# Mamba's gate: SiLU of z per channel tile, tanh on ScalarE and two GpSimd operations at written-out slots

## The chip, the core and the metric

The program runs on one core of a Trainium2 chip. The metric is the device time of one execution in microseconds (us); of the kernel before, the median of three runs is taken. The profile is one further execution with every instruction recorded. The engines are named as in the profile: PE (TensorE), with its weight loads as PEld; DVE (VectorE); ACT (ScalarE); POOL (GpSimd); and SP (SyncE), which issues the DMAs.

## The reference, cut to what matters

The input x has 64 x 64 positions (4096 tokens) of 256 channels, in float32. Three layers follow one another: a convolution and attention block, a bidirectional Mamba block with an MLP behind it, and a block of experts; each is added to its input. The change is in the second:

```python
def _mamba(x, ...):                       # once forward, once on the reversed tokens
    xz = einsum('bld,ed->ble', x, in_proj_w)
    xc, z = split(xz, 2, axis=-1)         # 512 channels each
    xc = silu(causal_conv(xc, conv_w, 4 taps) + conv_b)
    x_dbl = einsum('bld,ed->ble', xc, x_proj_w)    # dt (16), B (16 states), C (16)
    dt = softplus(einsum('blr,dr->bld', dt, dt_proj_w) + dt_proj_b)
    dA = exp(dt[..., None] * A)
    dBx = dt[..., None] * Bm[:, :, None, :] * xc[..., None]
    h_t = dA_t * h_{t-1} + dBx_t ;  y_t = sum over states of h_t * C_t
    y = y + xc * Dp
    y = y * silu(z)
    return einsum('bld,ed->ble', y, out_proj_w)

m = fwd + bwd
h = layernorm(m) * ln_g + ln_b
t = t + m + leaky_relu(h @ w1.T + b1, 0.01) @ w2.T + b2
```

silu(z) = z * sigmoid(z), which equals z/2 + z/2 * tanh(z/2).

## The kernel before, in words

The program has one phase for each layer. `mamba_phase` is the second and runs from about 2044 us to 4046 us of the span.

**Chunks and slots.** The 4096 tokens are cut into eight stretches of 512 (N), and each is gone through forward and backward, so there are 16 chunks, i = 0 to 15; even ones are forward (d = 0), odd ones backward (d = 1). A channel tile is 128 of the 512 channels (e = 0 to 3). The 16 states are cut into four quads (k). One tile of the scan has 128 partitions (32 channels by 4 states) and 2 x 512 elements. A chunk therefore has 4 (e) x 4 (k) x 2 (j) = 32 slots, and the phase 512. `at` is the slot's number in its chunk, 0 to 31.

**The order.** Everything in the phase is emitted in one written-out order: a loop over the slots emits, for slot n, its instructions to all engines, and each engine runs its own in that order and waits by semaphore for what it needs. Per slot n there are
- `inflow(n + 2)` on POOL (L1669): the product of dt*x and B for the slot two ahead, into one of three `dbx` buffers;
- `keep(n - 1)` on ACT (L1700): the last column of the scan before is copied out as state;
- `decay(n + 1)` on ACT (L1659): two exp of 128 x 512 into one of two PSUM buffers `da`;
- `bring(n + 1)` on ACT (L1692): from chunk 2 on, the state brought over from the chunk before is added to the first column of `dbx`;
- `recur(n)` on DVE: the scan (L1677) in place on `da`, and the product h with C (L1682);
- every second slot, `sum_states` on PE (L1709): the sums over states into `y`; at slots 8, 16, 24 and 0, `close` on DVE (L1717): y times silu(z) into the tile that held xc.

**Beside the slots.** `output` projects the finished chunk at slots 1 to 3 (L1434 on PE; ACT copies the result for forward chunks, L1439, and DVE adds it for backward ones, L1441). At slot 0 of a chunk ACT runs SiLU over its z, two tiles of 128 x 1024 (L1777); for chunk 0 this is done at the start (L1585).

`prepare(q)` is a generator that makes the inputs of the next chunk, one step a slot: the in-projection of xc (`in_pair`, PE L1250) at slots 29 and 30, copies on ACT (L1277, L1281) at 30 and 31, the four taps as matmuls (PE L1294) at slots 3 to 6, their bias on ACT (L1290) at 4 to 7, one SiLU over the whole xc at slot 8 (L1298), the projections to B, C and dt, an exp at slot 16, a log at slot 23 (L1342), and at slots 24 to 29 the pieces of dt on POOL: L1365 an addition and L1376 a product, each 128 x 512, whose results SP stores (L1380). The projections of z run at slots 24 and 26, and ACT copies them out of PSUM at 25 and 27 (L1355; for chunk 0 L1570). At slot 27 SP issues the load of the next chunk's input u (`load_u`, L1259). The last two pieces of dt come at slots 2 and 4 of the next chunk. SP issues every DMA of these in program order; `load_dt` fetches dt rows for the next channel tile (L1419).

`tail(c)` is a generator for one finished pair of chunks: LayerNorm (PE L113 and L122, DVE L116, ACT, POOL L132 and L138), an addition on POOL (L1457), the MLP (PE L1465, ACT, DVE L1471, PE L1476, DVE L1481), and the store with the token sums. It advances by at most one step a slot, and only if the slot is not in the set `FULL` of the engine that the step uses.

`few` is a ring of three 128 x 512 buffers; z tiles have three buffers of 128 x 1024.

Of the kernel before, what the change touches and what calls it, by code (L numbers as in the profile page):

```python
# [18 lines left out]
AF = mybir.ActivationFunctionType  # L19
ALU = mybir.AluOpType  # L20
# [1146 lines left out]
def mamba_phase(cx, early, w_in, w_x, w_out, w1, w2, x1d, ud, bcd, dtd, x2d, u2d, usum):  # L1167
# [11 lines left out]
    nc, tc = cx.nc, cx.tc  # L1179
    with ExitStack() as ctx:  # L1180
# [60 lines left out]
        def mm_psum():  # L1241
            return pmm.tile([P, N], FP, name="mm", tag="mm")
# [13 lines left out]
        def load_u(i):  # L1256
            c, d = divmod(i, 2)
            u = early.new_u()
            nc.sync.dma_start(out=u, in_=ud[NCH - 1 - c if d else c])  # L1259
            gots[i] = {"u": u}  # L1260

        def in_pair(q, e):
            return [in_proj(q % 2, gots[q]["u"], e), in_proj(q % 2, gots[q]["u"], e + 1)]

        def few():
            return sp.tile([P, N], FP, name="few", tag="few", bufs=3)

        def prepare(q):

            d, got = q % 2, gots[q]  # L1270

            ps = in_pair(q, 0)
            yield
            xp = early.wide("xp")
            nc.scalar.copy(xp[:, :, 0:3], halo[d])
            for v in range(2):
                nc.scalar.copy(xp[:, v, 3:], ps[v])  # L1277
            ps = in_pair(q, 2)
            yield
            for v in range(2):  # L1280
                nc.scalar.copy(xp[:, 2 + v, 3:], ps[v])  # L1281
            nc.scalar.copy(halo[d], xp[:, :, N : N + 3])
            for _ in range(4):
                yield

            xc = None
            for e in range(ET + 1):
                if e > 0:
                    xc = got["xc"] = xc or pr.tile([P, ET, N], FP, name="xc", tag="xc")
                    nc.scalar.activation(xc[:, e - 1, :], ps, AF.Identity, bias=cx.col(f"convb{d}", e - 1))  # L1290
                if e < ET:
                    ps = mm_psum()
                    for k in range(4):
                        nc.tensor.matmul(  # L1294
                            ps, taps[d][:, 4 * e + k, :], xp[:, e, k : k + N], start=k == 0, stop=k == 3
                        )
                yield
            nc.scalar.activation(xc, xc, AF.Silu)  # L1298
            yield
            ps = mm_psum()  # L1300
            nx = DR + 2 * DS
            for e in range(ET):
                nc.tensor.matmul(ps[0:nx, :], wx[d][:, e, :], xc[:, e, :], start=e == 0, stop=e == ET - 1)
            yield
            xd = few()[0:nx, :]
            nc.scalar.copy(xd, ps[0:nx, :])

            at = 0 if d else DR
            nc.sync.dma_start(out=bcd[q], in_=xd[at : at + 2 * DS, :])
            yield  # L1310


            r = slice(32 * d, 32 * d + DR)
            ex = dt = None
            for e in range(ET + 1):
                if e > 0:
                    ex = early.wide("ex")[:, :, 0:N] if e == 1 else ex
                    dt = dt or sp.tile([P, ET, N], FP, name="dt", tag="dt")
                    nc.scalar.activation(ex[:, e - 1, :], ps, AF.Abs, bias=cx.col(f"dtb{d}", e - 1))
                    nc.scalar.activation(dt[:, e - 1, :], ps, AF.Relu, bias=cx.col(f"dtb{d}", e - 1))  # L1320
                if e < ET:
                    ps = mm_psum()
                    nc.tensor.matmul(ps, wdt[r, P * e : P * e + P], xd[r, :], start=True, stop=True)
                yield

            nc.scalar.activation(ex, ex, AF.Exp, scale=-1.0)
            yield
            rds, sums = {}, {}
            for e in range(ET + 2):
                if e < ET:  # L1330
                    rd = rds[e] = few()
                    nc.scalar.activation(rd, ex[:, e, :], AF.Identity, scale=-1.0, bias=-1.0)
                    nc.scalar.add(rd, rd, 1.0)
                if e > 1:
                    nc.scalar.copy(dt[:, e - 2, :], sums.pop(e - 2))
                if 0 < e <= ET:
                    ps = sums[e - 1] = mm_psum()
                    for v, x in enumerate((rds.pop(e - 1), ex[:, e - 1, :], dt[:, e - 1, :])):
                        nc.tensor.matmul(ps, cx.ident, x, start=v == 0, stop=v == 2)
                yield  # L1340

            nc.scalar.activation(ex, ex, AF.Ln, bias=1.0)  # L1342
            yield
            got["dt"] = dt
            for at, (v, e) in enumerate(((0, 0), (1, 0), (0, 1), (1, 1), (0, 2), (0, 3))):
                dt_piece(q, v, e, ex)
                if at == 4 and q > 1:
                    load_first(q, 0)
                if at in (0, 2):
                    zs = in_pair(q, ET + at)  # L1350
                if at in (1, 3):
                    z = sp.tile([P, 2, N], FP, name="z", tag="z", bufs=3)
                    got.setdefault("z", []).append(z)
                    for f in range(2):
                        nc.scalar.copy(z[:, f, :], zs[f])  # L1355
                if at == 3 and q + 1 < 2 * NCH:
                    load_u(q + 1)
                yield

        def dt_piece(q, v, e, ex=None, eng=nc.gpsimd):  # L1360


            dt, xc = gots[q]["dt"], gots[q]["xc"]
            if v == 0:
                eng.tensor_tensor(dt[:, e, :], dt[:, e, :], ex[:, e, :], ALU.add)  # L1365
                if q < 2:
                    return
                if e == 0:
                    firsts[q] = ip.tile([P, ET], FP, name="first", tag="first", bufs=1)
                nc.gpsimd.tensor_tensor(firsts[q][:, e : e + 1], dt[:, e, 0:1], odd[:, 0:1], ALU.add)  # L1370
                if e % 2:
                    first_rows[q, e // 2] = cx.rows.tile([P, 2], FP, name="first_row", tag="first_row", bufs=2)
                    nc.sync.dma_start(out=first_rows[q, e // 2], in_=firsts[q][:, e - 1 : e + 1])
            else:
                x = few()
                eng.tensor_tensor(x, dt[:, e, :], xc[:, e, :], ALU.mult)  # L1376

                eng.tensor_tensor(dt[:, e, 0:1], dt[:, e, 0:1], odd[:, 1:2], ALU.add)
                for w, piece in enumerate((dt[:, e, :], x)):
                    nc.sync.dma_start(out=dtd[2 * q + w][e].rearrange("p j n -> (p j) n"), in_=piece)  # L1380

        def load_first(q, h):

# [107 lines left out]
        def start():  # L1491


            got, xp = gots[0], early.xp
# [42 lines left out]
            for v in range(2):  # L1537
                dt_piece(0, v, 0, ex, nc.vector)
# [19 lines left out]
            zs = in_pair(0, ET)  # L1558
# [7 lines left out]
            for h in range(2):  # L1566
                z = sp.tile([P, 2, N], FP, name="z", tag="z", bufs=3)
                got.setdefault("z", []).append(z)
                for f in range(2):
                    nc.scalar.copy(z[:, f, :], zs[f])  # L1570
                if h == 0:
                    zs = in_pair(0, ET + 2)
                    for v in range(2):
                        dt_piece(0, v, 1, ex)
                    yield
# [5 lines left out]
            yield  # L1581
            dt_piece(0, 1, 2)
            yield
            for z in got["z"]:
                nc.scalar.activation(z, z, AF.Silu)  # L1585
            dt_piece(0, 0, 3, ex)
            load_u(1)
            yield
# [60 lines left out]
        gots, bcs, dts, m_of, das, us, ys, hs = {}, {}, {}, {}, {}, {}, {}, {}  # L1649
# [65 lines left out]
        def close(i, e):  # L1715
            g, z = gots[i]["xc"], gots[i]["z"]
            nc.vector.tensor_tensor(g[:, e, :], ys.pop((i, e)), z[e // 2][:, e % 2, :], ALU.mult)  # L1717

        there = set()
        CARRY = {30: (0, 0), 31: (0, 2), 9: (1, 0), 11: (1, 2)}  # L1720

        AHEAD = 3
# [2 lines left out]

        FULL = {
            "PE": {0, 1, 2, 3, 4, 5, 6, 7, 9, 18, 19, 20, 21, 24, 26, 29, 30},
            "ACT": {0, 6, 7, 8, 16, 17, 18, 19, 20, 21, 22, 23, 30, 31},
            "POOL": {0, 1, 2, 4, 24, 25, 26, 27, 28, 29, 30, 31},
            "DVE": {8, 16},  # L1730
            "DMA": {},
        }
# [1 line left out]
        with tc.manual_schedule(engines=ORDERED):  # L1734
# [5 lines left out]
            for n, (i, e, k, j) in enumerate(slots):  # L1740
                at = n % SPS
                if at == 0:
                    prep, coming = coming, None
                if at in CARRY and 1 < i + (at > 16) < 2 * NCH:
                    carry(i + (at > 16), *CARRY[at])
                inflow(n + 2)
# [22 lines left out]
                if 1 <= at <= 3 and out is not None:  # L1769
                    step(out)  # L1770
                    if at == 3:
                        out = None
                        if (i - 1) % 2:
                            tails.append(tail((i - 1) // 2))
                if at == 0 and i > 0:
                    for z in gots[i]["z"]:
                        nc.scalar.activation(z, z, AF.Silu)  # L1777
                if i == 0:
                    step(begin)
                step(prep, LATE.get(at, 1) if i == 0 else 1)  # L1780
# [340 lines left out]
```

## Time and profile before

| | |
|---|---|
| runs | 4381.84 us median of 3 (4381.3 to 4389.78) |
| profiled execution | 4368.56 us, span 4366.8 us, mean granted PE clock 0.904 |
| phases in the span | convolutions to 760 us, attention to 2044, Mamba to 4046, experts to the end |
| Mamba window, 2002 us: busy | DVE 1893.0, PE 1619.0, ACT 1451.4, POOL 1449.4 |
| scan L1677 (512) and product L1682 (512) | 2.350 us and 1.225 us each |
| inflow L1669 (512), decay L1659 (1024) | 2.360 us on POOL, 0.692 us on ACT |
| SiLU of z: L1777 | 30 activations of 1.049 us, 15 table loads of 1.283 us |
| closing product L1717 (64) | 0.681 us |

Rows of a group of instructions read: line, engine, operation, out<-in with partitions x elements, count | busy us, mean ns of one | idle time of the engine in front of them and what ended it. Rows of the timeline read: start us, duration us, engine, line, operation, and in brackets the idle time just before and what ended it. Rows of waits read: who waited <- what ended the wait: us in total, times, longest us. Rows of windows read: window, its length, and the busy time of PE, PEld, DVE, ACT and POOL with their instruction counts, the granted PE clock, the DMA share and GB/s.

### The profile page before, as it was taken

To read this page: it belongs to the slowest core of one execution; us is meant where nothing else is said; L and a number is where in the kernel's file an instruction comes from. 1 tells how busy PE (TensorE), PEld (TensorE's weight loads), DVE (VectorE), ACT (ScalarE), POOL (GpSimd) and SP (SyncE) were. 2 spreads that over 40 slices of the span, in tenths; PEclk is the share of its full clock that TensorE was granted. 3 is DMA by queue.
4 is the path that set the end of the run, shared out by engine and by line. 5 is a ranking of instruction groups with operands and counts; after the bars stand their busy time and mean duration, and the time that the engine had idled before them with its cause. 6 is when DMAs were issued, how large, how long until landed. Compare 5 with 4: busy or idle time off the path is not lost. (4 is left out here: it accounts for less than half of the span.)

```text
span 4366.8 us, 43278 instructions
## 1 busy us (share of the span) xinstructions
PE 3693.8 (85%) x15072; PEld 1180.6 (27%) x15072; DVE 3600.9 (82%) x2976; ACT 2685.7 (62%) x4175; POOL 1563.3 (36%) x1051
## 2 busy tenths in 40 slices
PE   4659895999999999997878788888788788876698
PEld 2224341222222222222222222222222222221243
DVE  6887876888879879778899999999999999999311
ACT  1012223888788888776677777777777777774122
POOL 2210000000000000002677677776767777776000
PEclk9879996999999999998888989989888898977799
DMA  4322223000000000003332334443323334332121
GB/s 148 125 77 93 75 79 129 4 30 11 25 23 18 16 23 18 11 23 118 104 108 98 103 124 119 123 119 107 127 82 124 124 114 118 120 109 84 63 63 37
DMA packets 150243, 351.18 MB, mean 80 GB/s; under 512 B 35461, under 2 KB 44421, under 8 KB 149502
## 3 DMA queue, kind: packets, MB, share of 16 engines
q1 hardware_dynamic: 139214, 313.17, 23.1%
q0 software_dynamic: 10800, 35.14, 2.3%
q8 instruction: 120, 1.97, 0.2%
q14 instruction: 109, 0.89, 0.1%
HBM read 268.69 MB, written 79.56 MB: 80 GB/s over the span
## 5 line engine op out<-in xcount | busy, mean ns | idle before, releaser
L1669 POOL TENSOR_TENSOR dbx<-dtxr,b 128x1024 f32<-128x1024 f32 x512 | 1205.8, 2360 | 467.7 <-DVE da L1677 320.7
L1677 DVE TENSOR_TENSOR_SCAN da<-da,state,dbx 128x1024 f32<-128x1024 f32 x512 | 1203.2, 2350 | 62.0 <-ACT state L1700 33.6
L960 ACT ACTIVATE e<-sc 128x1024 f32<-128x1024 f32 x1024 | 992.8, 1023 | 204.7 <-PE sc L953 161.2
L881 DVE TENSOR_TENSOR s<-s,e 128x1024 f32<-128x1024 f32 x768 | 880.6, 1216 | 44.7 <-ACT e L960 44.2
L1659 ACT ACTIVATE da<-dtr,aneg 128x512 f32<-128x512 f32 x1024 | 708.3, 692 | 36.0 <-DMA dtr<-dtd 3.8
L953 PE MATMUL sc<-q,kS 32*128 32x512 f32 x4096 | 653.6, 644 | 20.4 <-DMA kS<-kd 11.4
L1682 DVE TENSOR_TENSOR h<-da,c 128x1024 f32<-128x1024 f32 x512 | 627.2, 1225 | 37.7
L888 PE MATMUL av<-e,vT 128*32 128x512 f32 x4096 | 549.8, 608 | 3.7 <-ACT o L894 3.7
L1709 PE MATMUL y<-h,sel 128*32 128x512 f32 x2048 | 442.0, 675 | 130.9 <-DVE h L1682 130.7
L132 POOL TENSOR_TENSOR ln_few<-ln_few,minus_half 128x4 f32<-128x4 f32 x29 | 29.4, 1015 | 1417.8 <-DMA ln_few<-ln_row 1417.8
L452 PE MATMUL cv<-v,u 128*128 128x512 f32 x928 | 422.2, 615 | 64.4 <-DVE pad L272 27.4
L953 PEld LDWEIGHTS sc<-q,kS 32*128 32x128 f32 x4096 | 211.3, 183 | 466.9 <-issue 244.4
L1250 PE MATMUL mm<-u,win 128*128 128x512 f32 x496 | 267.2, 688 | 72.0 <-DMA u<-ud 52.4
L1700 ACT COPY state<-da 128x2 f32<-128x2 f32 x511 | 80.5, 158 | 362.5 <-DVE h L1682 360.0
L452 PEld LDWEIGHTS cv<-v,u 128*128 128x128 f32 x928 | 182.1, 198 | 302.9 <-issue 230.9
L528 DVE SCALAR_TENSOR_TENSOR acc<-pad,wdw_s,acc 128x768 f32<-128x768 f32 (+1 forms) x192 | 244.5, 1279 | 19.4 <-ACT acc L524 13.3
L1294 PE MATMUL mm<-xp,taps 128*128 128x512 f32 x480 | 221.3, 609 | 6.0 <-DVE m L1441 5.1
L881 DVE TENSOR_TENSOR s<-e 128x1024 f32<-128x1024 f32 x128 | 150.8, 1219 | 71.6 <-ACT e L960 71.4
L888 PEld LDWEIGHTS av<-e,vT 128*32 128x32 f32 x4096 | 81.3, 108 | 396.6 <-issue 379.0
L1709 PEld LDWEIGHTS y<-h,sel 128*32 128x32 f32 x2048 | 60.4, 114 | 468.5 <-DVE h L1682 292.8
L1250 PEld LDWEIGHTS mm<-u,win 128*128 128x128 f32 x496 | 104.2, 221 | 244.8 <-issue 127.0
L504 ACT COPY pad<-pad 128x480 f32<-128x480 f32 x12 | 7.1, 594 | 214.2 <-DVE pad L272 214.1
(338 smaller groups left out, 3747.3 us busy)
## 6 DMA issues: line engine op xcount, KB each, us to landing
dtr<-dtd SPq DMA_DIRECT2D x128, 512.0 KB
dtxr<-dtd SPq DMA_DIRECT2D x128, 512.0 KB
b<-bcd SPq DMA_DIRECT2D x64, 256.0 KB
c<-bcd SPq DMA_DIRECT2D x64, 256.0 KB
dtd<-dt SPq DMA_DIRECT2D x64, 256.0 KB
dtd<-few SPq DMA_DIRECT2D x64, 256.0 KB
u<-uv SPq DMA_DIRECT2D x24, 640.0 KB
u<-ud SPq DMA_DIRECT2D x16, 512.0 KB
```

The source lines that it names most:

```text
L452: nc.tensor.matmul(rows4(ps), u[:, dy, P * ci : P * ci + P], v[:, dy : dy + HR, ci, :], start=dy + ci == 0, stop=dy == k - 1 and ci == CT - 1,
L528: nc.vector.scalar_tensor_tensor(o, src, w_ap, o, ALU.mult, ALU.add)
L881: nc.vector.tensor_tensor(z, x, y, ALU.add)
L888: nc.tensor.matmul(g.av[32 * h : 32 * h + 32, :], vT[:, kb, P * t + 32 * h : P * t + 32 * h + 32], es[h // 2][:, h % 2, :], start=kb == 0, ...
L953: nc.tensor.matmul(ps[h // 2][:, h % 2, :], kS[r, t, P * kb : P * kb + P], q_t[r, t, :], start=True, stop=True,)
L960: nc.scalar.activation(e, ps[i], AF.Exp)
L1250: nc.tensor.matmul(ps, win[d][:, t, P * e : P * e + P], u[:, t, ::-1] if d else u[:, t, :], start=t == 0, stop=t == CT - 1,)
L1659: nc.scalar.activation(da[:, v, :], dts[i, e, j][0][:, v, :], AF.Exp, scale=aneg[i % 2][:, a : a + 1])
L1669: nc.gpsimd.tensor_tensor(u, dts[i, e, j][1], bcs[i, k][0][:, None, :].to_broadcast([P, 2, N]), ALU.mult)
L1677: nc.vector.tensor_tensor_scan(da, da, u, state[i % 2][:, 4 * e + j, k : k + 1], ALU.mult, ALU.add)
L1682: nc.vector.tensor_tensor(h, da, bcs[i, k][1][:, None, :].to_broadcast([P, 2, N]), ALU.mult)
L1709: nc.tensor.matmul(ys[i, e][32 * j : 32 * j + 32, :], cx.sel, hs[n + j // 2][:, j % 2, :], start=False, stop=k == SQ - 1,)
```

## The change

z is halved as it is copied out of PSUM: `scalar.mul` by 0.5 in the place of `scalar.copy`, in `prepare` and for chunk 0. The two SiLU activations at slot 0 of every chunk, and those of chunk 0, are gone. In their place `swish` makes silu(z) from z/2 for one channel tile at a time, at fixed slots: tanh of 128 x 512 on ACT into a `few` buffer at slots 4, 11, 13 and 21; the product of it with z/2 on POOL at slots 6, 12, 15 and 22; and the addition of z/2 on POOL, into z, at slots 7, 14, 16 and 23. In a slot these come behind the inflow, the decays and the scan of the slot. The sets `FULL` change: ACT's free slots now include 0 and no longer 4, 11 and 13, and POOL's no longer 6, 7, 14, 15 and 22.

```diff
@@ prepare, and the start of chunk 0
                     for f in range(2):
-                        nc.scalar.copy(z[:, f, :], zs[f])
+                        nc.scalar.mul(z[:, f, :], zs[f], 0.5)
@@ new
+        def swish(i, at):
+
+            e, part = SWISH[at]
+            z = gots[i]["z"][e // 2][:, e % 2, :]
+            if part == 0:
+                tanhs[i, e] = few()
+                nc.scalar.activation(tanhs[i, e], z, AF.Tanh)
+            elif part == 1:
+                nc.gpsimd.tensor_tensor(tanhs[i, e], tanhs[i, e], z, ALU.mult)
+            else:
+                nc.gpsimd.tensor_tensor(z, z, tanhs.pop((i, e)), ALU.add)
@@ start of chunk 0
-            for z in got["z"]:
-                nc.scalar.activation(z, z, AF.Silu)
             dt_piece(0, 0, 3, ex)
@@ tables
+        SWISH = {
+            4: (0, 0), 6: (0, 1), 7: (0, 2), 11: (1, 0), 12: (1, 1), 14: (1, 2),
+            13: (2, 0), 15: (2, 1), 16: (2, 2), 21: (3, 0), 22: (3, 1), 23: (3, 2),
+        }
+        tanhs = {}
...
-            "ACT": {0, 6, 7, 8, 16, 17, 18, 19, 20, 21, 22, 23, 30, 31},
-            "POOL": {0, 1, 2, 4, 24, 25, 26, 27, 28, 29, 30, 31},
+            "ACT": {4, 6, 7, 8, 11, 13, 16, 17, 18, 19, 20, 21, 22, 23, 30, 31},
+            "POOL": {0, 1, 2, 4, 6, 7, 14, 15, 22, 24, 25, 26, 27, 28, 29, 30, 31},
@@ the loop over slots
-                if at == 0 and i > 0:
-                    for z in gots[i]["z"]:
-                        nc.scalar.activation(z, z, AF.Silu)
+                if at in SWISH:
+                    swish(i, at)
```

More of the change, by code (lines that the diff above doesn't have):

```diff
@@ L1569, in start @@
                 for f in range(2):
-                    nc.scalar.copy(z[:, f, :], zs[f])
+                    nc.scalar.mul(z[:, f, :], zs[f], 0.5)
                 if h == 0:
```

## The prediction

> **What bounds the kernel now.** I read the page's busy shares first, then the windows by phase, then the waits inside the Mamba phase, and last the timelines of single chunk starts. The change touches the Mamba phase alone (2044 to 4046 us), so that phase is read by itself.
>
> ```profile
> PE 3693.8 (85%) x15072; PEld 1180.6 (27%) x15072; DVE 3600.9 (82%) x2976; ACT 2685.7 (62%) x4175; POOL 1563.3 (36%) x1051
> 2044.00:4046.00 2002.00, 1619.03 (x4337) 499.20 (x4335) 1893.01 (x1171) 1451.38 (x2799) 1449.44 (x851) 0.87 0.36 112
> ```
>
> Over the whole span PE looks like the bound. In the Mamba window (columns PE, PEld, DVE, ACT, POOL) DVE is busy 1893.0 of 2002 us, PE 1619, ACT and POOL some 1450 each. Each of the 512 slots needs one scan (2.35 us) and one product (1.23 us) on DVE, so the phase's length is DVE's work plus DVE's gaps, about 109 us. Only work added to DVE or a change in those gaps moves the end. The waits in front of the scan:
>
> ```profile
> DVE da L1677 <- ACT state L1700: 33.6, 20, 2.7
> DVE da L1677 <- ACT dbx L1692: 13.5, 20, 3.3
> DVE da L1677 <- ACT da L1659: 11.0, 10, 3.9
> ```
>
> The largest ends with ACT's state copy, 20 times, at most 2.7 us. Its place is seen in a chunk start, here ACT in chunk 7, and DVE's scan behind it:
>
> ```profile
> 2927.47 1.28 ACT L1777 ACT_TABLE_LOAD   x1
> 2928.77 2.01 ACT L1777 ACTIVATE z<-z 128x1024 f32<-128x1024 f32 x2
> 2930.68 0.14 ACT L1700 COPY state<-da 128x2 f32<-128x2 f32 x1
> 2930.84 1.28 ACT L1659 ACT_TABLE_LOAD   x1
> 2932.13 1.42 ACT L1659 ACTIVATE da<-dtr,aneg 128x512 f32<-128x512 f32 x2
> ...
> 2933.80 2.36 DVE L1677 TENSOR_TENSOR_SCAN da<-da,state,dbx 128x1024 f32<-128x1024 f32 x1 [2.69 <-ACT state L1700]
> ```
>
> SiLU's table load, two activations and the load back to exp hold ACT for 4.6 us at slot 0, and the decays of slot 2 come behind them: the scan of slot 2 waits 2.69 us. Gap by gap, DVE stands in front of slot 2 for 27.3 us in 15 chunks: about 2.5 in each of chunks 1 to 5, 2.69 in 7, 9, 11 and 13, 0.5 in 6, 8, 10, 12 and 15, 1.12 in 14. Even chunks from 6 on have little, because DVE has the output additions of slots 2 and 3 and tail work to do there.
>
> **The change part by part.** The rows that price it:
>
> ```profile
> L1777 ACT ACTIVATE z<-z 128x1024 f32<-128x1024 f32 x30 | 30.1, 1049 | 0.2
> L1777 ACT ACT_TABLE_LOAD x15 | 19.2, 1283 | 0.3
> L1333 ACT ACTIVATE few<-few 128x512 f32<-128x512 f32 x60 | 37.8, 630 | 1.9
> L1355 ACT COPY z<-mm 128x512 f32<-128x512 f32 x60 | 32.7, 578 | 23.3 <-PE mm L1250 23.2
> L1376 POOL TENSOR_TENSOR few<-dt,xc 128x512 f32<-128x512 f32 x63 | 80.3, 1275 | 0.1
> ```
>
> ACT loses 32 SiLU activations (32 x 1.05 = 33.6 us) and, by the built order, 32 table loads (32 x 1.28 = 41.1); no load stands in front of a tanh there. It gains 64 tanh of 128x512, about 0.63 each as L1333 (40 us). No row has a tanh: 0.58 (a copy) to 0.69 (an exp) bound it, 37 to 44. The halving of z in its copy is an activation with a scale instead of a copy: 0 to 0.1 each (0.578 against 0.674 for L1290), 0 to 6 us. ACT falls by about 29 us; it is not the bound, so this pays only where DVE waits for it.
>
> POOL gains 128 operations of 128x512 by 1.18 to 1.28 us, 151 to 163 us on 1449 of 2002: it still fits, and the question is what lies behind each. Eight a chunk stand at slots 6, 7, 12, 14, 15, 16, 22 and 23, always behind the inflow of two slots ahead. Before slot 22 POOL idles for DVE (320.7 us of waits for the scan), so these six cost nothing while POOL keeps its two slots' lead. DVE never runs them, and no DMA is added. But changed free-slot sets push the tail (LayerNorm and MLP of a finished chunk pair) to other slots; from chunk 5 on, one begins at slot 27 of an even chunk, not at slot 11.
>
> *Gain at slot 2.* What is late next is PE. In chunk 7:
>
> ```profile
> 2932.15 3.70 PE L1434 MATMUL mm<-xc,wout 128*128 128x512 f32 x8
> 2936.00 3.70 PE L1294 MATMUL mm<-xp,taps 128*128 128x512 f32 x8 [0.15 <-ACT m L1439]
> 2939.63 1.05 PE L1709 MATMUL y<-h,sel 128*32 128x512 f32 x4
> 2940.99 1.05 PE L1709 MATMUL y<-h,sel 128*32 128x512 f32 x4 [0.31 <-DVE h L1682]
> 2941.97 7.14 PE L1294 MATMUL mm<-xp,taps 128*128 128x512 f32 x16
> ```
>
> From the in-projection through the output projection (L1434) to the last tap PE runs with only 0.15 + 0.31 us idle. The last tap releases the bias activations (L1290), then the SiLU of the whole xc at slot 8 (3.2 us with its load), then the decays of slot 10, for which the scan of slot 10 already waits 0.4 to 0.9 us in odd chunks. So DVE gains 2.69 at slot 2 there and waits for PE at slot 10. Following the built order from row to row I get 0.5 to 0.7 for chunks 5, 7, 9, 11 and 13 (3.1 together, and a variance product of 1.98 us now at slot 31 is counted in), and 1.6, 2.0, 1.9 and 1.8 for chunks 1 to 4, where the last taps end earlier against ACT (7.3). Chunk 15: 0.5 at slot 2 and 0.9 of y's at slot 8 (1.4). A stall of slot 29 in chunks 3, 7 and 11 shrinks by 0.2 each (0.6). At the end the token sums hide in a 2.17 us wait of DVE for PE (1.2). Gains: 3.1 + 7.3 + 1.4 + 0.6 + 1.2 = 13.6.
>
> *Loss at the chunk's end.* The add at slot 23 stands on POOL in front of the pieces of dt (L1365, L1376). From the landing of slot 25's dtxr, POOL runs back to back through slot 30 in the even chunk 2 (2389.8 to 2414.6). SP is queued in order: it issues the load of u (L1259) behind the stores of a piece, and PE waits for u, and ACT's copies, the decays and the next slot 0 wait for PE:
>
> ```profile
> 2416.02 6.20 PE L1250 MATMUL mm<-u,win 128*128 128x512 f32 x8 [7.93 <-DMA u<-ud]
> ...
> 2424.70 2.36 DVE L1677 TENSOR_TENSOR_SCAN da<-da,state,dbx 128x1024 f32<-128x1024 f32 x1 [3.34 <-ACT dbx L1692]
> ```
>
> At the ends of chunks 0, 1 and 2 nothing covers the 1.27: 3.8 us. At later odd ends PE's z projection gates, not POOL; at later even ends DVE has a LayerNorm subtraction (1.21) newly at slot 28, which covers the 1.27. Chunk 3 has a tail product (8 matmuls, about 3.6 us by L1476's rows) in front of the z projection: +2.0. In even chunks 6 to 14 the built order puts the last MLP product (again 8 matmuls) at slot 31, in front of the y sums of slots 30 and 31: the closing product (L1717) then waits about 1.3, less the 0.5 from slot 2, about +0.85 each, 4.3 for five. Rest +0.2. Losses: 3.8 + 2.0 + 4.3 + 0.2 = 10.3.
>
> That product may cost more, since it comes after PE has waited. The trace has such a case in the taps:
>
> ```profile
> 2567.39 5.40 PE L1294 MATMUL mm<-xp,taps 128*128 128x512 f32 x8 [2.22 <-DVE m L1441]
> ```
>
> 5.40 instead of 3.70 for the same eight, after 2.22 us of idling: up to +1.7 each, 8.5 in five chunks. I take 3.6, since PE's idle ahead of slot 31 is nearer to 0.5 to 1.4 us, and keep 8.5 for the range.
>
> The Trainium skill, TensorE: Matmul & The Clock Gate, "What's actually happening", has the clock fall to half only after an idle window of about 3.4 us. By that rule these eight would stay at 3.70 and the 8.5 would be nothing; the row above, with 2.22 us, speaks against the rule.
>
> Sum: 10.3 - 13.6 = -3.3 on the profiled execution's 4368.6, 4365.3. The runs' median is 13.3 above that execution, so 4378.5 stands for the median.
>
> **Rivals.**
>
> *F, PE doesn't hold the gain.* My figures at slots 2 to 10 rest on PE's modelled ends. If the chain has slack, DVE keeps the 27.3 of slot 2 instead of the 10.9 (7.3 + 3.1 + 0.5) and the 3.1 already inside the even chunks: 13.3 more, -16.6 in all, 4365.2. For it: ACT's work shrinks by 75 us at the very place of the longest wait. Against it: 0.46 us of idle on PE in chunk 7, and the slot-10 waits of today.
>
> *S, slower: the add at slot 23 delays u at every boundary.* If the LayerNorm subtraction doesn't cover it and the odd ends are POOL's too, 1.27 at 14 ends is 17.8 instead of 3.8: -3.3 + 14.0 = +10.7, 4392.5. It decides as soon as more than two or three further ends pay (3.3 / 1.27). For it: `mm<-u,win` waits 52.4 us for u over the phase, and POOL has no slack from slot 25 to 31. Against it: at odd ends PE's projections come last. With the slow product of slot 31 alone (+8.5) it is +5.2, 4387.0.
>
> *T, tanh needs a table of its own.* Then each tanh would bring a pair of loads, 64 x 2.57 = 164 us on ACT, some 100 us of it on the path. The built order has no such load (32 fewer in the executed half); I give it nothing.
>
> **How the numbers follow.** Walked sum 0.38, F 0.29, S with its variant 0.33. About 0.2% (8.7 us) is what a measurement of this kernel can tell from no change. The walked sum gives "same" in 0.24, faster in 0.07, slower in 0.07; F faster in 0.25, same 0.04; S slower in 0.27, same 0.04, and faster 0.02 where the rest errs the other way. So faster 0.34, same 0.32, slower 0.34. The range takes F with the ends' losses (5.8) at nothing, -22.4, 4359, and a little under it for halving and tanh at their low ends; and S with the slow product, 10.7 + 8.5 = +19.2, 4401: from 4357 to 4402. The walked sum's own range is 4368 to 4390.
>
> **What would show it.** Right: no table load at slot 0; the wait of the scan for the state copy falls from 33.6 to under 10, the scans of slot 10 wait longer (for the decays), and POOL is busy near 1600 us in the phase. F would show as no new waits at slot 10; S as more than 52.4 us of PE waiting for u and more than 13.5 us of scans waiting for the brought-in state. Wrong it would be if POOL lost its two-slot lead in the middle of a chunk (scans waiting for dbx, 3.8 us today), or if DVE ran its products slower beside a busier POOL: 1% on 512 x 3.58 us is 18 us by itself.

## The result and the profile after

The changed kernel takes 4404.18 us (median of 6 runs, 4397.54 to 4408.44) against 4383.98 for the kernel before (6 runs): a ratio of 1.0044, with a 95% interval of 1.0033 to 1.0054. It is 20 us slower. The predicted time was 4378.5, the range 4357 to 4402; the median lies two us above the range, and the likeliest case had the other sign.

In the profiled executions the span goes from 4366.8 to 4395.7 us. Of these 29 us, 7.4 lie ahead of the first Mamba scan (2048.4 against 2055.8), some 5 of them in the phases before it, which the change doesn't touch; 19.3 lie between the first and the last scan; 2.3 come behind. The profile of before lies 15 us below the median of its six runs, the one of after 7 below. A single profile's total is therefore good to some 15 us here, and below the prices come from timed runs while the profiles tell where the time lies. The page of after, and the Mamba window (PE, PEld, DVE, ACT, POOL):

```profile
PE 3669.3 (83%) x15072; PEld 1180.9 (27%) x15072; DVE 3605.4 (82%) x2976; ACT 2652.7 (60%) x4175; POOL 1712.9 (39%) x1179
2051.00:4073.00 2022.00, 1589.00 (x4334) 496.69 (x4333) 1894.78 (x1170) 1417.67 (x2799) 1598.04 (x979) 0.87 0.37 111
```

DVE does the same work (1894.8 us against 1893.0), ACT has 34 us less, POOL 149 more: the engines' sums are as forecast. The window is 20 us longer all the same, so it is DVE's gaps. The groups that are new:

```profile
L1388 ACT ACTIVATE few<-z 128x512 f32<-128x512 f32 x64 | 39.2, 613 | 0.0
L1355 ACT ACTIVATE z<-mm 128x512 f32<-128x512 f32 x60 | 33.6, 585 | 14.3 <-PE mm L1250 14.2
L1390 POOL TENSOR_TENSOR few<-few,z 128x512 f32<-128x512 f32 x64 | 81.3, 1270 | 0.0
L1392 POOL TENSOR_TENSOR z<-z,few 128x512 f32<-128x512 f32 x64 | 81.2, 1269 | 0.0
```

The terms for the operations were right: tanh 0.613 us (0.63 taken), the halving copy 0.585 (0.58 to 0.67), POOL's two 1.27 each, and no table load in front of any of the 64 tanh. The waits of the Mamba phase (who waited <- what ended it: total, times, longest) show what changed; lines 1380 to 1582 of the old kernel are 12 higher in the new, lines 1585 to 1720 are 10 higher. First the kernel before:

```profile
PE mm L1250 <- DMA u<-ud: 52.4, 13, 7.9
...
DVE xc L1717 <- PE y L1709: 6.7, 4, 3.2
...
DVE ln_xc L116 <- PE tl L113: 1.6, 4, 0.4
...
ACT dbx L1692 <- POOL dbx L1669: 0.7, 2, 0.3
```

The changed kernel:

```profile
DVE xc L1727 <- PE y L1719: 33.2, 20, 3.3
DVE da L1687 <- ACT dbx L1702: 20.1, 15, 4.6
DVE da L1687 <- ACT da L1669: 19.9, 9, 3.8
DVE ln_xc L116 <- PE tl L113: 10.5, 5, 2.6
DVE da L1687 <- ACT state L1710: 3.6, 8, 0.8
...
PE mm L1250 <- DMA u<-ud: 66.2, 12, 8.9
ACT dbx L1702 <- POOL dbx L1679: 21.8, 17, 3.2
```

The scan's wait for the state copy is gone (33.6 to 3.6), as intended. In its place stand waits of the closing product for PE (6.7 to 33.2 us), of the tail's LayerNorm subtraction for PE (1.6 to 10.5), and longer waits of the scan for the decays and the brought-in state. DVE's idle time in front of its instructions, added up by slot from its timeline over all chunks (two profiles of each kernel, us; a timeline row shows gaps above 0.15 us):

```
slot        0     1     2     8     10    11    16    29    slots 0 to 30
before      10.9  3.8   27.3  7.9   3.4   0     0.6   6.5   69.1
again       10.6  4.4   33.1  6.8   4.7   0     0.6   6.0   77.0
after       34.0  1.0   0     5.1   17.6  10.6  10.9  1.0   88.3
again       33.7  1.3   0     4.7   16.6  8.1   12.1  1.3   86.4
```

Slot 2 gives its 27 to 33 us back, and slots 0, 10, 11 and 16 take 55 to 58. In all the gaps grow by 19 us in the first pair of profiles and by 9 in the second.

### The profile page after: what moved, and what is told of

It is laid out like the page before. It is cut to its first block, busy times and chain, and to the rows that moved or that the text cites. A ratio compares the mean times of both kernels' runs of the same rounds, so it can differ in the third digit from the quotient of the medians.

```text
span 4395.7 us, 43458 instructions
## 1 busy us (share of the span) xinstructions
PE 3669.3 (83%) x15072; PEld 1180.9 (27%) x15072; DVE 3605.4 (82%) x2976; ACT 2652.7 (60%) x4175; POOL 1712.9 (39%) x1179
## 5 line engine op out<-in xcount | busy, mean ns | idle before, releaser
L1687 DVE TENSOR_TENSOR_SCAN da<-da,state,dbx 128x1024 f32<-128x1024 f32 x512 | 1203.1, 2350 | 45.0 <-ACT dbx L1702 20.1
L1692 DVE TENSOR_TENSOR h<-da,c 128x1024 f32<-128x1024 f32 x512 | 627.2, 1225 | 37.7 <-DVE da L1687 0.9
L1250 PE MATMUL mm<-u,win 128*128 128x512 f32 x496 | 276.3, 708 | 91.3 <-DMA u<-ud 66.2
L1702 ACT ACTIVATE dbx<-dbx,brought 128x1 f32<-128x1 f32 x448 | 125.2, 280 | 22.4 <-POOL dbx L1679 21.8
```

The source lines that it names most:

```text
L1250: nc.tensor.matmul(ps, win[d][:, t, P * e : P * e + P], u[:, t, ::-1] if d else u[:, t, :], start=t == 0, stop=t == CT - 1,)
L1687: nc.vector.tensor_tensor_scan(da, da, u, state[i % 2][:, 4 * e + j, k : k + 1], ALU.mult, ALU.add)
L1692: nc.vector.tensor_tensor(h, da, bcs[i, k][1][:, None, :].to_broadcast([P, 2, N]), ALU.mult)
```

## The experiments

Three suspects: the tail's steps, which the new free-slot sets move; POOL's new work, above all the addition at slot 23; and PE's chain at slot 10, which in the prediction kept most of the gain from being had. Each kernel is compared with runs of the kernel before on the same chip, since that kernel's medians lay between 4372 and 4385 in the several sets of runs; ratios carry their 95% interval.

### The tail back at its old slots

```diff
-            "ACT": {4, 6, 7, 8, 11, 13, 16, 17, ...},
-            "POOL": {0, 1, 2, 4, 6, 7, 14, 15, 22, 24, ...},
+            "ACT": {0, 6, 7, 8, 16, 17, ...},
+            "POOL": {0, 1, 2, 4, 24, ...},
```

> The changed kernel with the free-slot sets of the kernel before, so that the tail's steps stand where they stood. Theory 1, the moved tail: DVE's waits of the changed kernel for PE at slot 0 (17 us), slot 11 (10.5) and slot 16 (10.3) belong to the moved tail and go, 38 us of gaps; the 27 us of slot 2 stay won, some 14 of them are given back at slot 10, and a few us are lost at slot 0: 5 to 12 us faster than the kernel before. Theory 2, the added POOL work (the add of slot 23 in front of the pieces of dt and the load of u): it is still there, 8 us or more slower than before.

Measured: 4375.8 us against 4384.9, ratio 0.9978 (0.9968 to 0.9988). The changed operations with the old sets are 9 us faster than before; the sets alone turn that into 20 us slower. In the profile the closing product waits 6.0 us for PE in place of 33.2, and the gaps at slots 11 and 16 fall to 0 and 0.7. Theory 1, the moved tail, holds: the tail's slots cost 29 us in the changed kernel, give or take 6 by the two intervals.

How they cost it is seen in the changed kernel's timelines, PE and DVE at the start of chunk 8:

```profile
3049.73 3.70 PE L1250 MATMUL mm<-u,win 128*128 128x512 f32 x8
3053.26 1.88 PE L1488 MATMUL tl<-a1a,w2s 128*128 128x512 f32 x4
3054.98 1.88 PE L1488 MATMUL tl<-a1b,w2s 128*128 128x512 f32 x4
3056.79 1.06 PE L1719 MATMUL y<-h,sel 128*32 128x512 f32 x8
...
3053.74 1.23 DVE L1692 TENSOR_TENSOR h<-da,c 128x1024 f32<-128x1024 f32 x1
3057.92 0.69 DVE L1727 TENSOR_TENSOR xc<-y,z 128x512 f32<-128x512 f32 x1 [2.96 <-PE y L1719]
```

A product of the MLP's second layer (L1488, slot 31 of chunk 7) stands on PE in front of the y sums of slots 30 and 31, and DVE's closing product waits 2.96 us for them. At slot 11 of the same chunk:

```profile
3099.89 1.23 DVE L1692 TENSOR_TENSOR h<-da,c 128x1024 f32<-128x1024 f32 x1
3103.71 1.22 DVE L116 TENSOR_TENSOR ln_xc<-m,tl 128x1024 f32<-128x1024 f32 x1 [2.60 <-PE tl L113]
...
3096.07 3.63 PE L1303 MATMUL mm<-xc,wx 128*48 128x512 f32 x8
3099.64 1.12 PE L1717 MATMUL y<-xc,skip 128*128 128x512 f32 x2
3100.69 1.06 PE L1719 MATMUL y<-h,sel 128*32 128x512 f32 x8
3101.69 1.98 PE L113 MATMUL tl<-m,mean_mat 128*128 128x512 f32 x4
```

The mean (L113) is emitted at slot 10 and the subtraction that needs it at slot 11, while PE is still at the projection to B, C and dt. DVE stands in order, so slot 12's scan waits with it. In odd chunks the first-layer product of slot 15 stands likewise in front of slot 16's y sums.

### Only ACT's set back

```diff
-            "ACT": {4, 6, 7, 8, 11, 13, 16, 17, ...},
+            "ACT": {0, 6, 7, 8, 16, 17, ...},
```

> The changed kernel with ACT's free slots of before alone; POOL's stay the new ones. By the built order the tail then stands where it stood before, but for one POOL product at slot 8 in place of 6. If ACT's two barred slots, 11 and 13, are what moved the tail, the time is that of the kernel with both old sets, 5 to 12 us faster than before; if POOL's set matters as much, it stays 5 us or more slower than before.

Measured: 4372.9 us against 4383.8, ratio 0.9977 (0.9965 to 0.9990), that is the time with both sets back. So it is ACT's set that moved the tail, and POOL's cost nothing measurable. By the built order it is the bars on slots 11 and 13, put there to make room for a tanh of 0.6 us: with these two lifted every matmul and LayerNorm subtraction of the tail stands where it stood, while the bar on slot 4 and the freeing of slot 0 move nothing.

### The new sets alone, and three kernels without SiLU

The kernel before, with only the new sets (run twice):

> The kernel before, with the SiLU of z at slot 0, and only the free-slot sets changed. Theory 1: the waits at slots 0, 11 and 16 appear although POOL and ACT have no new work, 20 to 38 us slower than before. Theory 2: no POOL work was added, so within 5 us of before.

> The kernel before with only the new free-slot sets, once more: its profiled execution was the slowest of its runs. If the moved tail costs little as long as the SiLU at slot 0 stands, again 3 to 10 us slower than before; if the first result was low by chance, 15 or more.

Measured: ratios 1.0013 (1.0003 to 1.0022) and 1.0018 (1.0008 to 1.0027): 6 and 10 us slower. The waits at slots 0, 11 and 16 are there (the closing product waits 30 to 34 us for PE), so they come from the sets and not from POOL's work; but they cost a fifth to a third of the 29 us. So the sets' cost depends on what else stands in the kernel. The next kernels leave SiLU of z out altogether, at slot 0 as shown and at the start of chunk 0, twice with the old sets and once with the new:

```diff
-                if at == 0 and i > 0:
-                    for z in gots[i]["z"]:
-                        nc.scalar.activation(z, z, AF.Silu)
```

> The kernel before without any SiLU of z (y is multiplied by z itself, so the gate is left out of the computation). It shows what the removal at slot 0 is worth when nothing else moves. If PE's chain to the taps holds the scan of slot 10, most of the 27 us of slot 2 comes back as a longer wait there: 8 to 15 us faster than before. If PE doesn't hold it: 25 us or more faster.

> The kernel before without any SiLU of z (the gate is z itself), once more, as the base for the next kernel on the same chip: 25 to 35 us faster than before.

> Without any SiLU of z, and with the new free-slot sets: the moved tail alone, where no stall of slot 2 is left. If the stall of slot 2 hides part of the moved tail's waits in the kernel with SiLU (ACT's late decays are covered by DVE's wait for PE at slot 0), the same sets cost 20 us or more here against the kernel without SiLU and with the old sets, not 6. If the large cost in the changed kernel comes from POOL's new work meeting the moved tail, they cost 6 us here too.

Measured: without SiLU, ratios 0.9920 (0.9904 to 0.9937) and 0.9914 (0.9898 to 0.9931), 35 us faster than before both times. With the new sets besides, 0.9987 (0.9975 to 0.9998): 4372.7 against 4343.8 on the same chip, so the sets cost 29 us here, with no new POOL work in the kernel at all, and 10 us with SiLU on that chip. That rules out POOL's work as the partner of the moved tail. The likely partner is the stall of slot 2, as a cover: with SiLU at slot 0 DVE waits anyway, and waits that the moved tail adds ahead of slot 2 are partly that same wait. The kernel with the new sets alone shows a part of it: slot 2's gaps fall from 27 to 33 us to 22 in both its profiles, in the even chunks 4 to 14 to at most 0.2, from 0.5 to 2.7. That accounts for 5 to 11 of the some 20 us; the rest is not shown. DVE's gaps (the last column of the table, means of the profiles at hand) grow by 13 us through the new sets with SiLU, from 73 to 86, and by the same 13 without, from 45 to 59. So the difference between 10 and 29 us stands on the timed runs alone. The profiled executions are a poor sample of it: without SiLU the second one with the old sets was the slowest of its four runs, and the one with the new sets the fastest of its ten.

### POOL's last addition, one slot earlier

```diff
-                if at in SWISH:
+                if at in SWISH and at != 23:
                     swish(i, at)
+                if at == 22:
+                    swish(i, 23)
```

> The changed kernel with POOL's last addition of each chunk at slot 22, in front of the inflow that waits for slot 25's dtxr, and not behind it at slot 23. Everything else, the tail's slots too, stays. Theory 2: PE's wait for u (66 us) falls to about the 52 of before, and the time by 8 us or more. Theory 1: PE's wait for u falls, but the time by 6 us at most, against the changed kernel's 4404.

Measured: 4389.0, ratio 1.0012 (1.0001 to 1.0022), against 1.0044 for the change as it was: 14 us. In front of the inflow of slot 25, POOL waits for a DMA anyway, and the addition fits into that wait; behind it, it delays the pieces of dt and the load of u. Chunk 12, first in the changed kernel, then in this one:

```profile
3658.24 2.35 POOL L1679 TENSOR_TENSOR dbx<-dtxr,b 128x1024 f32<-128x1024 f32 x1 [2.67 <-DMA dtxr<-dtd]
3660.54 1.28 POOL L1392 TENSOR_TENSOR z<-z,few 128x512 f32<-128x512 f32 x1
...
3642.16 1.26 POOL L1392 TENSOR_TENSOR z<-z,few 128x512 f32<-128x512 f32 x1
3644.93 4.66 POOL L1679 TENSOR_TENSOR dbx<-dtxr,b 128x1024 f32<-128x1024 f32 x2 [1.51 <-DMA dtxr<-dtd]
```

PE's wait for u and the scan's for the brought-in state, in this kernel:

```profile
PE mm L1250 <- DMA u<-ud: 47.3, 11, 7.3
...
DVE da L1687 <- ACT dbx L1702: 10.8, 13, 2.4
```

They were 66.2 and 20.1 (59.1 and 15.6 in the second profile), and DVE's gaps at slot 0 fall from 34.0 to 22.0 us (slot 10's rise from 17.6 to 23.9 in this profile). So one POOL operation of 1.27 us, 16 times, cost some 14 us, about 0.9 each.

### Both repairs

> The changed kernel with both: the free-slot sets of before and the last addition of a chunk at slot 22. If the two losses are separate (28 us for the tail's slots and 15 us for the addition, from the single runs), they add up: 4376 - 15 = 4361, some 24 us faster than before. If the late u only hurts with the moved tail, 4370 to 4376.

Measured: 4352.7 against 4372.0, ratio 0.9953 (0.9935 to 0.9971), 19 us faster than before. With the old sets the earlier addition takes slot 0's gaps from 23.9 to 12.0 us and leaves slot 10's at 17. The addition is worth 0.0025 (11 us) here and 0.0032 with the moved tail; within the intervals the two losses are separate and add up.

### The first tile's operations at slots 0, 1 and 3

In addition to both repairs:

```diff
+        EARLY = {0: 4, 1: 6, 3: 7}
...
+                if at in SWISH and at != 23 and (i == 0 or at > 7):
                     swish(i, at)
+                if i > 0 and at in EARLY:
+                    swish(i, EARLY[at])
```

> As the kernel of the two repairs (sets of before, last addition at slot 22), and the tanh, product and addition of the first channel tile at slots 0, 1 and 3, from chunk 1 on, where the change has them at 4, 6 and 7. If POOL's product and addition at slots 6 and 7 delay slot 10's inflow, and with it the SiLU of xc that ACT issues behind the state brought over at slot 8, then DVE's gaps at slot 10 fall from about 17 us to about 7, as without SiLU, and the time by 8 to 12 us against the kernel of the two repairs. If PE's chain holds slot 10, nothing changes there.

Measured: 4348.4, ratio 0.9946 (0.9929 to 0.9962), 4.4 us faster than with both repairs on the same chip, where 8 to 12 were expected. With four runs of each (4347.3 to 4350.6 against 4347.9 to 4355.2) this difference is not clear of noise. The gaps at slot 10 do fall, from 17.3 to 8.8 us, but slot 29 (4.3 to 7.0) and slot 13 (0 to 1.4) take some back. The reason for slot 10's gaps is visible in chunk 7 of the changed kernel with the old sets, first POOL, then ACT:

```profile
2952.58 2.35 POOL L1679 TENSOR_TENSOR dbx<-dtxr,b 128x1024 f32<-128x1024 f32 x1 [2.31 <-DMA dtxr<-dtd]
2954.90 1.27 POOL L1392 TENSOR_TENSOR z<-z,few 128x512 f32<-128x512 f32 x1
2956.12 2.36 POOL L1679 TENSOR_TENSOR dbx<-dtxr,b 128x1024 f32<-128x1024 f32 x1
...
2954.18 0.69 ACT L1290 ACTIVATE xc<-mm,small 128x512 f32<-128x512 f32 x1 [1.24 <-PE mm L1294]
2954.76 0.15 ACT L1710 COPY state<-da 128x2 f32<-128x2 f32 x1
2954.95 1.42 ACT L1669 ACTIVATE da<-dtr,aneg 128x512 f32<-128x512 f32 x2
2956.30 0.28 ACT L1702 ACTIVATE dbx<-dbx,brought 128x1 f32<-128x1 f32 x1
2958.51 0.29 ACT L1702 ACTIVATE dbx<-dbx,brought 128x1 f32<-128x1 f32 x1 [1.93 <-POOL dbx L1679]
2958.81 1.28 ACT L1298 ACT_TABLE_LOAD   x1
```

At slot 8 ACT brings the state into slots 9 and 10, and so waits for slot 10's inflow, which POOL is given in that same slot. POOL's lead of two slots is no lead there, and the addition of slot 7 (L1392) stands in front of it, behind an inflow that had itself waited 2.31 us for a DMA. Behind the wait on ACT come the SiLU of xc and the decays of slot 10. The last bias of the taps (L1290) was done 3.9 us before the table load of that SiLU: POOL, not PE, is what it waits for. The waits of ACT for POOL, first with the two repairs, then in this kernel:

```profile
ACT dbx L1702 <- POOL dbx L1679: 18.5, 14, 2.4
...
ACT dbx L1702 <- POOL dbx L1679: 6.0, 8, 1.5
```

### A second profile of each kernel

> The kernel before itself, for a second profile: the first one's execution (4368.6) lies under every later run of that kernel (4375 to 4394). If the loads of u land later in other executions, DVE's gaps in front of slot 0 sum to more than the 10.9 us of the first profile, some 20 us; if the first profile is typical, they stay within 3 us of 10.9.

> The changed kernel itself, for a second profile: the gaps of DVE at slots 0, 11 and 16 are again some 35, 10 and 10 us, each within 3 us.

They are in the table above. Slot 0 of the kernel before is 10.6 again, so the late u is no matter of one execution; slot 2 is 33.1 there, so the stall that the change takes away was larger in this execution than in the one that the prediction was made from. After's gaps are the same within 3 us.

## Why the prediction was wrong

**The gain at slot 2, 13.6 us: too small, and its mechanism wrong.** The step was that PE's chain to the last tap leaves no room and slot 10 takes the gain back. Taking SiLU out and moving nothing gave 35 us; slot 10's gaps were 6.5 and 5.4 us there, against 3.4 and 4.7. In chunk 7 of the kernel without SiLU the last bias of the taps is waited for by ACT for 1.24 us, but ACT then waits 1.32 us for POOL's inflow before the SiLU of xc: the chain on PE isn't what ends last.

```profile
2944.73 0.69 ACT L1290 ACTIVATE xc<-mm,small 128x512 f32<-128x512 f32 x1 [1.24 <-PE mm L1294]
...
2948.46 0.29 ACT L1690 ACTIVATE dbx<-dbx,brought 128x1 f32<-128x1 f32 x1 [1.32 <-POOL dbx L1667]
2948.76 1.28 ACT L1298 ACT_TABLE_LOAD   x1
```

A busy chain had been read as a chain with no slack. F, with the whole stall won, was right on this term.

**POOL's six operations before slot 22, costed at nothing: some 4 us for the two at slots 6 and 7, not clear of noise.** The cover named was POOL's two-slot lead. At slot 8 the order has ACT wait for an inflow that is issued in the same slot, and there the addition of slot 7 is on the path; the product of slot 6 comes ahead of POOL's wait for the DMA. The four at slots 12 to 16 were not tried apart. The wait (ACT for POOL) was in the trace at 0.7 us, and the prediction didn't look at whose lead ends where.

**The addition at slot 23, 3.8 us: measured 11 to 14.** The chain POOL, store, load of u, PE, slot 0 was right. Its size was nearer S's (1.27 at 14 ends is 17.8): the covers that were named, a subtraction on DVE at slot 28 and PE's projections at odd ends, hid less than was taken.

**The moved tail, 6.5 us: measured 29.** That is the step that failed most. The product at slot 31 was priced at 1.3 us of waiting, five times (by the built order it stands in the odd chunks 5 to 13, in front of the closing products at the starts of the even ones); the closing product waits 1.24 to 2.96 there, and 1.24 to 1.25 at the starts of chunks 7, 9, 11 and 13, behind the variance product, which had been taken as part of a small gain. The subtraction at slot 11 (8 to 10.6 us) and the first-layer product in front of slot 16's sums (10.9 and 12.1 us) were not priced at all, though the built order showed both: mean at slot 10 and subtraction at 11, with PE at the wide projection of slot 9. The cost was also taken as if it could be read off by adding waits; by the timed runs it is 6 to 10 us while SiLU stands at slot 0, and 29 once it is gone. That the change took away the cover of the waits it added fits this, and is shown in part, at slot 2.

**The end, a gain of 1.2 us: as forecast.** The token sums' reduction of 1.21 us (L1500) now stands behind the last closing product, and the addition that follows (L1613) starts 8.56 us after the start of the last scan in both kernels. Further on, from the last scan to the end of the span it takes 326.8 to 328.8 us in the profiles with the old sets and 327.5 to 329.9 with the new; a loss of up to 2 us there has no explanation here.

**Rivals.** The truth is F and S together with a tail cost that neither had: about -35 for the stall, +26 for the new operations (35 less 9 from the old sets' kernel; 11 to 14 for the addition at 23, some 4 for slots 6 and 7, the rest not settled) and +29 for the tail, which is +20. The sum came near zero in the prediction because its gain (13.6 of 35) and its losses (10.3 of 55) were both too small, so that it came as near as 26 us to the result is luck. The even chances of faster and slower were the better part of it; the range ended 2 us short. T is refuted: no load stands in front of a tanh. That DVE would run slower beside a busier POOL is refuted: the scan takes 2350 ns and the product 1225 in both profiles.

**The clock.** The product of slot 31 took 3.6 us and not 5.4: in chunk 8 it follows the in-projection without idling (1.88 and 1.88 above), and the price of 8.5 was not paid. Another tail product was slow. The four matmuls of slot 15 in chunk 7 came after 5.75 us of idling and took 3.78 us, at a granted clock of 0.50. The four of slot 25 came after 2.24 us and took 1.98, at 1.00:

```profile
2989.21 3.78 PE L1477 MATMUL tl<-hn,w1s 128*128 128x512 f32 x4 [5.75 <-DVE a1a L1483]
2992.92 1.10 PE L1719 MATMUL y<-h,sel 128*32 128x512 f32 x8
...
2994.16 0.69 DVE L1727 TENSOR_TENSOR xc<-y,z 128x512 f32<-128x512 f32 x1 [1.42 <-PE y L1719]
...
3028.65 1.98 PE L1477 MATMUL tl<-hn,w1s 128*128 128x512 f32 x4 [2.24 <-DVE a1a L1483]
...
2989.30:2992.80 3.50, 3.50 (x4) 1.08 (x4) 3.35 (x2) 2.85 (x5) 3.50 (x3) 0.50 0.00 0
3028.60:3030.60 2.00, 1.95 (x5) 0.99 (x6) 2.00 (x1) 1.17 (x3) 2.00 (x2) 1.00 0.88 305
```

The slow one is in front of slot 16's sums, and the closing product pays 1.42 us. The prediction's row stands too: its eight matmuls took 5.40 us after 2.22 us of idling, and the kernel before has the granted clock at 0.50 there:

```profile
2567.90:2571.20 3.30, 3.30 (x5) 1.35 (x4) 3.27 (x3) 0.97 (x4) 2.51 (x3) 0.50 0.39 148
```

So pauses of nearly the same length, 2.22 and 2.24 us, were followed once by a slow clock and once by a full one; the length of the pause just in front doesn't settle the price.

The 29 us are not split among slots 0, 11 and 16 by times: an order that keeps the tail's PE steps off slot 31 alone ends in a deadlock, and gave no time.

## What to carry to other kernels

Moving one operation of a hand-written order to a free place can cost more than the operation, if a table of free slots moves other work with it: two barred slots for 0.6 us of ACT cost 29 us here, and the same tanh, products and additions with the old table and four of the twelve in a chunk earlier make the kernel 0.54% faster than before in place of 0.44% slower. A stall that is removed can have been the cover of what waits ahead of it, so price added waits as if the stall were already gone: the same table cost 6 to 10 us with it and 29 without. And a busy engine ahead of a wait proves no bound: leave the suspected work out once, and see what comes back.

## What was not expected of the hardware

The kernel before scatters by 19 us, 4375 to 4394 over 25 runs on one chip. The kernel without SiLU of z stays within 3 and 5 us on two chips, but with only four runs on each, and with the new sets besides it spreads over 15 us in ten runs. So whether the stall makes the scatter is open. The profile from which the prediction was made lay 15 us below the median of six runs of that kernel.
